# A hybrid of state-space scan, attention and mixture of experts: an attention order table, small transfers for the diagonals, a last product by chunk, and list products behind their codes

## The chip, the cores and the metric

The kernel runs on one core of a Trainium2 chip, as one launch. The metric is the device time of that launch in microseconds (us); less is better. The core has five instruction streams that run side by side and wait for each other by semaphores: TensorE (PE in the profile, its weight loads PEld), VectorE (DVE), ScalarE (ACT), GpSimd (POOL) and SyncE (SP). Each takes its own instructions in the order in which they were emitted. Nearly all plain transfers are issued from SP's queue, a few from ACT's, and gathers and scatters from POOL's.

## The reference, cut to what matters

The input is four images of 32x32 positions with 256 channels, in float32; in the reference below the tokens of an image are its 1024 positions.

```python
# layer 0: norm, projection to 512 channels, 3x3 depthwise convolution, gelu, selective scan
x = layernorm(src) @ w_in + b_in
x = gelu(depthwise_conv3x3(x) + conv_b)
dt_raw, B, C = split(x @ w_x)                 # 16, 64 and 64 columns
dt = softplus(dt_raw @ w_dt + dt_bias)
for t in tokens:                              # h: 512 channels x 64 states
    h = exp(dt[t] * A) * h + (dt[t] * x[t]) * B[t]
    y[t] = sum over the 64 states of h * C[t]
x = src + layernorm(y + x * D_skip) @ w_out + b_out
# layer 1: attention without a softmax over tokens, then experts
q, k, v = split(layernorm(t) @ W_qkv + b_qkv)  # q, k centred, squared and normalised to q2, k2
t = t + (v + q2 @ (k2.T @ v) / sqrt(N)) @ W_out + b_out
p = softmax(layernorm(t) @ gate_w + gate_b); the best two of 16 experts per token
t = t + sum of the two: weight * (silu(z @ w1) * (z @ w2)) @ w3
```

## The kernel before, in words

**Scan.** Layer 0 is cut into eight units, each half an image (512 tokens), and each unit into 64 steps, one for each state `n`. A step has four slots, one for each chunk `m` of 128 channels. In a slot ACT makes the decay `da` (`decay`), PE turns `dt*x*B` into a PSUM bank (`turn`), DVE runs the recurrence over 512 tokens (`scan`, L954), and PE adds the products with `C` up in PSUM (`add_up`, L975), eleven slots later (`LAG`). The product with `C` is one POOL instruction for all four chunks of a step (L961). The rows of `C`, called `cb_n`, are fetched three steps ahead by SP into four buffers (`fetch`, L880). The values that the next half image starts from go out by SP in a small transfer `last<-h` (L966). The work for the next units (norm, projection, convolution, `dt`) is fed into the slots from lists of pieces with a planned slot, which `beside` makes and the big loop under `tc.manual_schedule()` hands out.

The factor `B` can be multiplied in by ACT (`scale`), by POOL (`scale_apart`), or, for the first 128 tokens of some steps, by PE with a diagonal matrix. For that there are two DRAM tensors `diag_b[0]` and `diag_b[1]`, each 64 x 128 x 128. They are filled with zeros once (`zero_diagonals`, L252, in slots 4 and 14 of the first unit), and for each later unit `put_bc` writes the 64 x 128 entries of the diagonals, of 4 bytes each (L505). `fetch_diagonal` loads single matrices of it from the second unit on.

**Attention.** Layer 1 starts when the last scan has left PSUM. The order of its steps is a table, `ORDER`, of names with a batch and an index, which is run from front to back once; since every engine takes its instructions in the order of emission, the table sets each engine's order. The names that matter here:

- `st` are the statistics of one group of 128 tokens (DVE), `sc` scales half a batch by them (ACT, after a reciprocal on DVE), `tx` transposes it (PE), `qk` makes q and k (PE, then DVE and ACT), `vo` the part with v, `kv`, `ko`, `nk`, `kw` the matrix k2.T v and its scaling, `ou` the product with q2 and the statistics behind it.
- `ei` normalises half a batch for the experts into the tile `xe` (one buffer) and stores it to the DRAM tensor `xd` from SP; `te` and `ga` give the gate logits; `tg` and the `rs` steps choose the experts of a batch and find each token's place, a few DVE instructions each time; the weights of a batch's tokens go to `xd` from SP in one of them.
- `wr` writes a batch's rows to the output from ACT's queue. `nw` loads the weights of two experts into the memory of the finished batches' tiles `tb0`, `tb1`, `tb2` (names `m`), six transfers of 512 KB from SP in the order tb0, tb0, tb2, tb1, tb1, tb2. `fw` loads those of the first expert. `so` finishes the lists of the first three batches and gathers the first three blocks of rows.

**Experts.** The tokens are handled in 73 blocks of 128 rows (`blocks_of`). A block takes two halves of the hidden layer, 16 small matmuls each, named `p`, and two results `pf` (`hidden`, `result`). Beside the first eight blocks the rest of the routing is fed in, four pieces after each half block: `more_places` counts the blocks that experts with many tokens need beyond the fixed ones, and `more_rows` finds their rows. For these, DVE and ACT make a 0/1 `code` for eight groups of tokens at a time, eight codes in all, and PE multiplies each with the table `qh` in eight small matmuls (L2130). `more_places` also transposes a column `ef` on PE (L2085) from which DVE makes the expert numbers `eid`.

Of the kernel before, what the change touches and what calls it, by code (L numbers as in the profile page):

```python
# [22 lines left out]
def over_middle(ap, n):  # L23

    return ap.unsqueeze(1).to_broadcast([ap.shape[0], n, ap.shape[1]])
# [8 lines left out]
def conv_ssm_attn_moe_kernel(ctx: ExitStack, tc: tile.TileContext, a: dict, out: bass.AP):  # L34
# [110 lines left out]
    with ExitStack() as l0:  # L145
# [105 lines left out]
        def zero_diagonals(k):  # L251
            nc.sync.dma_start(  # L252
                out=diag_b[k].rearrange("n a b -> a n b"), in_=over_middle(zero, NS)
            )
# [200 lines left out]
        def dt_bc(w, needs):  # L455
# [42 lines left out]
            def put_bc():  # L498
                t = pre.tile([P, BANK], F32, name="bct")
                (nc.scalar.copy if on_scalar("bc") else nc.vector.tensor_copy)(t, made["bg"])  # L500
                cd = dram0.tile([NS, BANK], F32, name="cd")
                nc.sync.dma_start(out=cd, in_=t[NS:, :])
                if w > 0:
                    with nc.allow_non_contiguous_dma(reason="diagonals"):
                        nc.sync.dma_start(  # L505
                            out=diag_b[w % 2].rearrange("n a b -> n (a b)")[:, :: P + 1],
                            in_=t[:NS, :P],
                        )
                made["cd", w] = cd

# [125 lines left out]
            return parts + [todo]  # L636

# [308 lines left out]
        def scan(s, m):  # L946
# [12 lines left out]
            if m == DK - 1:  # L959
# [35 lines left out]
        def beside(u):  # L995
# [27 lines left out]
            if u + 1 < n:  # L1023
                lists.append(list(zip(dt_bc(u + 1, ("st", u - 1) if u > 0 else None), dts)))
            else:
# [67 lines left out]
        with tc.manual_schedule():  # L1093
# [14 lines left out]
            for k in range(n_all + LAG):  # L1108
# [13 lines left out]
                if k in (4, 14):  # L1122
                    zero_diagonals(1 if k == 4 else 0)
# [676 lines left out]
    def put_rows_out(b):  # L1800
# [14 lines left out]
        ('st', 0, 0), ('st', 0, 6), ('lt', 0), ('lt', 1), ('st', 0, 5), ('st', 0, 2), ('lp', 0),  # L1815
        ('lt', 2), ('st', 0, 1), ('st', 0, 3), ('sc', 0, 0), ('st', 0, 4), ('st', 0, 7),
        ('st', 1, 0), ('st', 1, 1), ('lp', 1), ('st', 1, 4), ('lt', 3), ('lp', 2), ('tx', 0, 0),
        ('lp', 3), ('sc', 0, 1), ('qk', 0, 0), ('st', 1, 2), ('tx', 0, 1), ('st', 1, 3),
        ('sc', 1, 0), ('qk', 0, 2), ('st', 1, 5), ('qk', 0, 5), ('qk', 0, 1), ('qk', 0, 3),
        ('f4', 0, 5), ('f4', 0, 0), ('st', 1, 6), ('qk', 0, 4), ('st', 1, 7), ('vo', 0, 0),  # L1820
        ('f4', 0, 2), ('f4', 0, 4), ('vo', 0, 4), ('k2', 0, 0), ('qk', 0, 6), ('tx', 1, 0),
        ('sc', 1, 1), ('f4', 0, 1), ('qk', 0, 7), ('vo', 0, 1), ('f4', 0, 7), ('tq', 0, 0),
        ('f4', 0, 3), ('st', 2, 0), ('f4', 0, 6), ('k2', 0, 1), ('st', 2, 5), ('qk', 1, 0),
        ('st', 2, 1), ('st', 2, 7), ('qk', 1, 1), ('tq', 0, 1), ('qk', 1, 2), ('f4', 1, 2),
        ('vo', 0, 2), ('st', 2, 2), ('ll',), ('tx', 1, 1), ('f4', 1, 0), ('kv', 0, 0),
        ('vo', 0, 7), ('st', 2, 6), ('qk', 1, 3), ('qk', 1, 4), ('vo', 0, 5), ('st', 2, 3),
        ('nq', 0), ('st', 2, 4), ('qk', 1, 5), ('kv', 0, 1), ('ls',), ('ko', 0), ('nk', 0),
        ('k2', 1, 0), ('kw', 0), ('co', 1), ('vo', 1, 1), ('sc', 2, 2), ('vo', 0, 6),
        ('ou', 0, 0), ('ou', 0, 1), ('vo', 0, 3), ('f4', 1, 1), ('ou', 0, 2), ('tx', 2, 0),
        ('qk', 1, 6), ('ou', 0, 3), ('f4', 1, 4), ('ou', 0, 6), ('vo', 1, 0), ('r3', 0),  # L1830
        ('ei', 0, 0), ('ou', 0, 4), ('f4', 1, 5), ('qk', 1, 7), ('st', 3, 0), ('f4', 1, 6),
        ('ou', 0, 7), ('k2', 1, 1), ('st', 3, 5), ('tq', 1, 0), ('ou', 0, 5), ('kv', 1, 0),
        ('f4', 1, 3), ('tq', 1, 1), ('wr', 0), ('f4', 1, 7), ('nq', 1), ('ei', 0, 1),
        ('qk', 2, 0), ('tx', 2, 1), ('vo', 1, 2), ('te', 0, 0), ('qk', 2, 1), ('st', 3, 1),
        ('te', 0, 1), ('st', 3, 2), ('f4', 2, 0), ('co', 0), ('st', 3, 6), ('ga', 0, 0),
        ('ga', 0, 1), ('st', 3, 4), ('vo', 1, 3), ('nk', 1), ('tg', 0), ('st', 3, 7), ('rs', 0),
        ('qk', 2, 2), ('kv', 1, 1), ('rs', 0), ('st', 3, 3), ('rs', 0), ('ko', 1), ('sc', 3, 2),
        ('rs', 0), ('vo', 1, 6), ('qk', 2, 3), ('f4', 2, 2), ('rs', 0), ('rs', 0), ('kw', 1),
        ('qk', 2, 4), ('f4', 2, 1), ('vo', 1, 4), ('rs', 0), ('ou', 1, 0), ('k2', 2, 0),
        ('rs', 0), ('f4', 2, 3), ('ou', 1, 2), ('qk', 2, 6), ('rs', 0), ('rs', 0), ('rs', 0),  # L1840
        ('ou', 1, 3), ('ou', 1, 4), ('vo', 2, 1), ('qk', 2, 5), ('ou', 1, 1), ('qk', 2, 7),
        ('vo', 1, 7), ('r3', 1), ('ei', 1, 0), ('k2', 2, 1), ('vo', 1, 5), ('f4', 2, 5),
        ('tx', 3, 0), ('rs', 0), ('ou', 1, 5), ('ou', 1, 7), ('rs', 0), ('vo', 2, 0), ('rs', 0),
        ('f4', 2, 4), ('vo', 2, 2), ('f4', 2, 7), ('rs', 0), ('te', 1, 0), ('kv', 2, 0),
        ('tq', 2, 0), ('rs', 0), ('ou', 1, 6), ('f4', 2, 6), ('qk', 3, 0), ('qk', 3, 1),
        ('tq', 2, 1), ('ei', 1, 1), ('vo', 2, 7), ('qk', 3, 2), ('ga', 1, 0), ('te', 1, 1),
        ('rs', 0), ('rs', 0), ('rs', 0), ('rs', 0), ('rs', 0), ('ga', 1, 1), ('tx', 3, 1),
        ('tg', 1), ('vo', 2, 4), ('rs', 1), ('rs', 1), ('rs', 0), ('rs', 1), ('wr', 1),
        ('kv', 2, 1), ('f4', 3, 0), ('rs', 1), ('ko', 2), ('nq', 2), ('nk', 2), ('rs', 1),
        ('qk', 3, 5), ('rs', 1), ('f4', 3, 1), ('rs', 1), ('kw', 2), ('qk', 3, 3), ('f4', 3, 3),  # L1850
        ('ou', 2, 0), ('vo', 2, 3), ('rs', 1), ('ou', 2, 4), ('qk', 3, 4), ('rs', 1),
        ('ou', 2, 1), ('k2', 3, 0), ('f4', 3, 4), ('ou', 2, 3), ('ou', 2, 2), ('rs', 1),
        ('r3', 2), ('qk', 3, 7), ('rs', 1), ('rs', 0), ('ei', 2, 0), ('vo', 2, 5), ('qk', 3, 6),
        ('rs', 1), ('ou', 2, 7), ('vo', 2, 6), ('ou', 2, 5), ('te', 2, 0), ('ou', 2, 6),
        ('f4', 3, 7), ('tq', 3, 0), ('ei', 2, 1), ('ga', 2, 0), ('rs', 1), ('vo', 3, 1),
        ('tq', 3, 1), ('f4', 3, 6), ('fw', 'w3'), ('rs', 1), ('vo', 3, 0), ('te', 2, 1),
        ('f4', 3, 2), ('k2', 3, 1), ('rs', 1), ('f4', 3, 5), ('rs', 1), ('rs', 1), ('vo', 3, 2),
        ('nq', 3), ('rs', 1), ('ga', 2, 1), ('kv', 3, 0), ('tg', 2), ('rs', 1), ('rs', 2),
        ('rs', 2), ('rs', 2), ('rs', 2), ('kv', 3, 1), ('nw',), ('ko', 3), ('wr', 2), ('rs', 2),
        ('rs', 2), ('rs', 2), ('rs', 2), ('nk', 3), ('fw', 'w2'), ('vo', 3, 4), ('rs', 2),  # L1860
# [203 lines left out]
    def more_places():  # L2064
# [37 lines left out]
        )  # L2102
        nc.vector.tensor_tensor(bh, bf, few, ALU.add)
        yield

    def more_rows(lo, hi):

        n = hi - lo
# [91 lines left out]
```

## Time and profile before

| | |
|---|---|
| median of 3 runs | 3352.31 us (3351.57 to 3356.69) |
| the profiled execution | 3350.39 us |
| its span, first to last instruction | 3348.6 us |
| PE, DVE, ACT, POOL busy | 3163.7, 2891.9, 2717.2, 2717.1 us |
| mean granted TensorE clock | 0.990 of full speed |

The busy times are unions over the span, and they are averages over stages with different limits. By the traces of the single instructions, the head of layer 0 lies at 0 to 128 us, the scan at 128 to 2682 us, attention at 2682 to 2910 us, and the experts from 2910 us to the end. In the profile's rows an engine is followed by the line of the kernel, the operation, the tile written and the tiles read, a count, the busy time and the idle time before it with the instruction or transfer that ended it. A granted clock of 1.00 is full speed.

### The profile page before, as it was taken

The numbers are of one execution on the slowest core, as the hardware profiler recorded it, in microseconds if no ns is written. First come the engines' busy times: TensorE is split into PE (matmuls) and PEld (weight loads), VectorE is DVE, ScalarE is ACT, GpSimd is POOL, SyncE is SP. The second block draws the span as 40 slices with busy tenths as digits, with TensorE's granted clock in tenths as the row PEclk, the third lists the DMA queues.
The fourth block names the chain that finished last, engine by engine and source line by source line (L and its number), as shares of the span: only waits on it lengthen the run. The fifth ranks groups of instructions, "written<-read, shape, count | busy, mean of one in ns | idle before, by whom it ended". The sixth has DMA issues, their size and how long they took to land. (4 is left out here: it accounts for less than half of the span.)

```text
span 3348.6 us, 62734 instructions
## 1 busy us (share of the span) xinstructions
PE 3163.7 (94%) x23407; PEld 2752.2 (82%) x23407; DVE 2891.9 (86%) x3435; ACT 2717.2 (81%) x4621; POOL 2717.1 (81%) x1215
## 2 busy tenths in 40 slices
PE   7899999999999999999999999989999999889998
PEld 4588888988899888888989888768778766689998
DVE  4699999999999999999999999999999978752222
ACT  1699999999999999999999999999999855422221
POOL 0388998999999989999999999999999943334443
PEclk9999999999999999999999999999999999899999
DMA  3542223224333232243333222422212121567785
GB/s 106 150 72 64 68 67 69 71 70 62 68 78 71 72 67 75 63 66 72 75 74 68 69 66 60 73 55 70 62 58 68 54 84 32 171 178 230 216 250 149
DMA packets 423835, 300.76 MB, mean 90 GB/s; under 512 B 225073, under 2 KB 329393, under 8 KB 423522
## 3 DMA queue, kind: packets, MB, share of 16 engines
q1 hardware_dynamic: 397202, 274.25, 31.8%
q0 software_dynamic: 14016, 18.05, 2.9%
q10 hardware_dynamic: 12304, 4.37, 0.5%
q8 instruction: 187, 3.06, 0.4%
q14 instruction: 126, 1.03, 0.1%
HBM read 262.34 MB, written 34.87 MB: 89 GB/s over the span
## 5 line engine op out<-in xcount | busy, mean ns | idle before, releaser
L961 POOL TENSOR_TENSOR h<-h,cb_n 128x2048 f32<-128x2048 f32 x512 | 2148.6, 4207 | 128.0 <-DVE h L954 79.7
L928 ACT ACTIVATE da<-dt,l_conv_a_log_sb 128x512 f32<-128x512 f32 x2048 | 1435.1, 712 | 21.1 <-DVE h L954 19.7
L908 ACT ACTIVATE bx<-dtxT,proj 128x512 f32<-128x512 f32 x1748 | 1243.4, 712 | 28.4 <-DVE dtxT L600 16.2
L975 PE MATMUL y<-ident,h 128*128 128x128 f32 x8192 | 1236.5, 274 | 9.1 <-POOL h L961 6.3
L954 DVE TENSOR_TENSOR_SCAN h<-da,last,ps 128x512 f32<-128x512 f32 x1024 | 1218.0, 1258 | 8.2 <-PE ps L940 2.8
L954 DVE TENSOR_TENSOR_SCAN h<-da,ps 128x512 f32<-128x512 f32 x1024 | 1169.4, 1200 | 30.3 <-ACT da L928 13.1
L940 PE MATMUL ps<-ident,bx 128*128 128x128 f32 x6992 | 1119.0, 276 | 39.9 <-DVE h L954 28.3
L975 PEld LDWEIGHTS y<-ident,h 128*128 128x128 f32 x8192 | 979.1, 141 | 99.9 <-issue 20.3
L940 PEld LDWEIGHTS ps<-ident,bx 128*128 128x128 f32 x6992 | 820.3, 142 | 99.3 <-DVE h L954 79.2
L1965 DVE TENSOR_TENSOR hT<-s,p 128x256 f32<-128x256 f32 x146 | 61.3, 420 | 282.3 <-ACT s L1964 282.3
L1983 POOL DMA_INDIRECT out_dram<-yb,src x73 | 116.0, 1589 | 211.1 <-DVE yb L1980 85.1
L940 PE MATMUL ps<-ident,bxp 128*128 128x128 f32 x800 | 236.7, 296 | 50.2 <-DVE h L954 37.3
L1964 ACT ACTIVATE s<-p 128x256 f32<-128x256 f32 x146 | 55.9, 383 | 267.0 <-PE p L1958 264.3
L413 PE MATMUL bg<-pad,dgc 128*128 128x256 f32 x864 | 258.2, 380 | 0.6 <-DMA dgc<-diags 0.6
L940 PEld LDWEIGHTS ps<-ident,bxp 128*128 128x128 f32 x800 | 112.0, 140 | 132.4 <-DVE h L954 78.9
L935 PE MATMUL ps<-dgb,dtxT 128*128 128x128 f32 x800 | 171.3, 296 | 21.6 <-DMA dgb<-diag_b 10.7
L919 POOL TENSOR_SCALAR bxp<-dtxT,proj 128x512 f32<-128x512 f32 x200 | 141.4, 707 | 58.8 <-DVE dtxT L600 58.8
L1958 PE MATMUL p<-xT,w 128*128 128x128 f32 x1408 | 173.4, 277 | 2.2 <-ACT xT L1938 2.2
L1958 PEld LDWEIGHTS p<-xT,w 128*128 128x128 f32 x1408 | 169.1, 193 | 5.2 <-ACT xT L1938 3.0
L935 PEld LDWEIGHTS ps<-dgb,dtxT 128*128 128x128 f32 x800 | 120.8, 191 | 48.9 <-DVE h L954 34.8
L413 PEld LDWEIGHTS bg<-pad,dgc 128*128 128x128 f32 x864 | 130.5, 191 | 0.8 <-DMA dgc<-diags 0.8
L1958 PE MATMUL p<-xT,m 128*128 128x128 f32 x928 | 115.3, 278 | 0.0
(342 smaller groups left out, 2671.9 us busy)
## 6 DMA issues: line engine op xcount, KB each, us to landing
cb_n<-cd SPq DMA_DIRECT2D x512, 256.0 KB, 3.3
m<-in_L_ffn_w_dram SPq DMA_DIRECT2D x87, 512.0 KB, 5.5
w<-in_L_ffn_w_dram SPq DMA_DIRECT2D x60, 512.0 KB, 7.3
dgc<-diags SPq DMA_DIRECT2D x84, 192.0 KB, 3.2
diag_b<-zero SPq DMA_DIRECT2D x2, 4096.0 KB, 16.6
dgb<-diag_b SPq DMA_DIRECT2D x100, 64.0 KB, 3.1
last<-h SPq DMA_DIRECT2D x256, 2.0 KB, 3.0
xd<-xe SPq DMA_DIRECT2D x8, 512.0 KB, 3.6
```

What stands on the lines that cost most here:

```text
L413: nc.tensor.matmul(made["bg"].rearrange("p (h w) -> p h w", w=WW)[:, blk(c, deep), :], made["dgc", m * 3 + i][:, j, :], pads[m][:, at : at ...
L908: nc.scalar.activation(t, made["dtxT", u][:, j, :], AF.Copy, scale=made["proj", u][:, j, R + n : R + n + 1])
L919: nc.gpsimd.tensor_scalar(t, made["dtxT", u][:, 0, :], made["proj", u][:, 0, R + n : R + n + 1], 1.0, ALU.mult, ALU.mult,)
L928: nc.scalar.activation(t, made["dt", u][:, m, :], AF.Exp, scale=A[:, m, n : n + 1])
L935: nc.tensor.matmul(t[:, blk(j, P)], made["dtxT", steps[s][0]][:, j, blk(m, P)], made["dgb", s], start=True, stop=True,)
L940: nc.tensor.transpose(t[:, blk(j, P)], made["bx", s, j][:, blk(m, P)], ident)
L954: nc.vector.tensor_tensor_scan(h[:, m, 1:], made.pop(("da", s, m)), made.pop(("dbx", s, m)), 0.0 if seg == 0 else last[b][:, n, m : m + 1] ...
L961: nc.gpsimd.tensor_tensor(h[:, :, :BANK], h[:, :, 1:], over_middle(made["c", s], DK), ALU.mult)
L975: nc.tensor.matmul(made["y", u][j][:, blk(m, P)], made["h", s][:, m, blk(j, P)], ident, is_transpose=True, start=n == 0 and m == 0, stop=n ...
L1958: nc.tensor.matmul(p12[:, j, s, :], w_of(w, key)[:, ck, blk(h + j, P)], on_b["xT", key][:, ck, :], start=(ck == 0), stop=(ck == CK - 1),)
L1965: nc.vector.tensor_tensor(on_b["hT", key][:, h : h + 2, :], s, p12[:, :, 1, :], ALU.mult)
L1983: s = nc.gpsimd.indirect_dma_start(of[:, :], bass.IndirectOffsetOnAxis(src[:, c : c + 1], 0), yb, None, bounds_check=NB * L - 1, oob_is_er ...
```

## The change

1. The zeros of the two diagonal tensors are written in sixteen transfers of eight matrices (512 KB) instead of two of 64 (4 MB), one in each of the first sixteen steps, those of `diag_b[1]` first.
2. The entries of a unit's diagonals are written in eight transfers of 8 x 128 elements instead of one of 64 x 128. They are pieces of their own, spread over the 40 slots from the planned start of `dt1`.
3. In the very last step of the scan, the product with `C` is made chunk by chunk, chunks 0 and 2 on POOL and 1 and 3 on DVE.
4. `ORDER` holds the same 332 entries in another order.
5. In `more_places` the transpose of `ef` and the making of `eid` come three pieces later, and in `more_rows` the matmuls of a code follow three codes behind it (`LATE`), with five buffers for the codes instead of two.

```diff
-        def zero_diagonals(k):
+        part_of = NS // 8
+
+        def zero_part(i):
+            k, n = 1 - i // 8, (i % 8) * part_of
             nc.sync.dma_start(
-                out=diag_b[k].rearrange("n a b -> a n b"), in_=over_middle(zero, NS)
+                out=diag_b[k][n : n + part_of].rearrange("n a b -> a n b"),
+                in_=over_middle(zero, part_of),
             )
...
-                if w > 0:
-                    with nc.allow_non_contiguous_dma(reason="diagonals"):
-                        nc.sync.dma_start(
-                            out=diag_b[w % 2].rearrange("n a b -> n (a b)")[:, :: P + 1],
-                            in_=t[:NS, :P],
-                        )
+                made["bct", w] = t
                 made["cd", w] = cd
+                done.add(("bct", w))
...
+        def entries(w):
+            def part(i):
+                with nc.allow_non_contiguous_dma(reason="diagonals"):
+                    nc.sync.dma_start(
+                        out=diag_b[w % 2].rearrange("n a b -> n (a b)")[
+                            blk(i, part_of), :: P + 1
+                        ],
+                        in_=made["bct", w][blk(i, part_of), :P],
+                    )
+            return [piece(4, "SP", 0, lambda i=i: part(i), need=("bct", w)) for i in range(8)]
...
-            if m == DK - 1:
+            if s + 1 == len(steps):
+                (nc.vector if m % 2 else nc.gpsimd).tensor_tensor(
+                    h[:, m, :BANK], h[:, m, 1:], made["c", s], ALU.mult
+                )
+            elif m == DK - 1:
...
+                lists.append([(entries(u + 1), (at["dt1"][0], at["dt1"][0] + 40))])
...
-                if k in (4, 14):
-                    zero_diagonals(1 if k == 4 else 0)
+                if k % DK == 2 and k // DK < 16:
+                    zero_part(k // DK)
...
     ORDER = (
-        ('st', 0, 0), ('st', 0, 6), ('lt', 0), ('lt', 1), ('st', 0, 5), ('st', 0, 2), ('lp', 0),
-        ('lt', 2), ('st', 0, 1), ('st', 0, 3), ('sc', 0, 0), ('st', 0, 4), ('st', 0, 7),
+        ('st', 0, 0), ('lt', 0), ('st', 0, 6), ('st', 0, 1), ('st', 0, 5), ('lt', 1),
+        ('st', 0, 2), ('st', 0, 3), ('lp', 0), ('st', 1, 0), ('lt', 2), ('sc', 0, 0), ('lp', 1),
...
-        ('nq', 3), ('rs', 1), ('ga', 2, 1), ('kv', 3, 0), ('tg', 2), ('rs', 1), ('rs', 2),
-        ('rs', 2), ('rs', 2), ('rs', 2), ('kv', 3, 1), ('nw',), ('ko', 3), ('wr', 2), ('rs', 2),
+        ('k2', 3, 0), ('nw',), ('rs', 1), ('vo', 2, 3), ('ou', 2, 3), ('qk', 3, 7), ('ou', 2, 2),
...
+        ('rs', 2), ('rs', 2), ('wr', 2), ('kv', 3, 1), ('ko', 3), ('rs', 1), ('rs', 2),
...
     )
...
         nc.vector.tensor_reduce(ef, done, AX.X, ALU.add)
-        pe = one()
-        nc.tensor.transpose(pe[:1, :P], ef, ident)
-        nc.vector.tensor_scalar(eid, pe[:1, :NMORE], float(NE - 1), None, ALU.min)
         yield
...
+            if k == 3:
+                pe = one()
+                nc.tensor.transpose(pe[:1, :P], ef, ident)
+                nc.vector.tensor_scalar(
+                    eid, pe[:1, :NMORE], float(NE - 1), None, ALU.min
+                )
             yield
...
+    LATE = 3
+
     def more_rows(lo, hi):
...
+        behind = []
+        def add_rows(k, c, code):
+            for j in range(GC):
+                nc.tensor.matmul(...)
...
                 yield
-                for j in range(GC):
-                    nc.tensor.matmul(...)
+                behind.append((k, c, code))
+                if len(behind) > LATE:
+                    add_rows(*behind.pop(0))
+        yield
+        for one_code in behind:
+            add_rows(*one_code)
```

## The prediction

> **What bounds the kernel now.** I read the page, then the engines' busy times by stage, then the waits and the time lines at the places that the edits touch.
>
> ```profile
> core 0: us, PE busy (x) PEld busy (x) DVE busy (x) ACT busy (x) POOL busy (x), PEclk, DMA share, GB/s
> 128.00:2682.00 2554.00, 2429.97 (x19000) 2157.93 (x19000) 2506.79 (x2299) 2475.31 (x3990) 2430.23 (x885) 1.00 0.30 70
> 2682.00:2910.00 228.00, 207.88 (x924) 144.01 (x923) 179.60 (x490) 117.87 (x358) 86.92 (x91) 0.97 0.26 82
> 2910.00:2980.00 70.00, 60.71 (x461) 54.91 (x462) 39.15 (x140) 19.41 (x43) 23.43 (x27) 0.92 0.66 186
> 2980.00:3338.00 358.00, 356.84 (x2710) 339.67 (x2708) 100.88 (x325) 73.22 (x193) 165.90 (x189) 1.00 0.75 218
> ```
>
> Each stage has its own limit. In the scan four engines are over 95% busy and DVE, at 98%, leads. Attention is PE's, at 91% with DVE behind. The first 70 us of the experts leave PE idle for 9.3 us at a clock of 0.92; after that PE has no room. So an edit pays where it closes a gap of the scan's DVE and ACT, of the join between scan and attention, or of PE at 2910 to 2980 us.
>
> **1. Zeros and entries.** SP's time line in the first steps of the scan:
>
> ```profile
> 133.78 0.62 SPq L252 DMA_DIRECT2D diag_b<-zero  x1
> 137.32 10.27 SPq L880 DMA_DIRECT2D cb_n<-cd  x1
> ...
> 151.56 0.57 SPq L252 DMA_DIRECT2D diag_b<-zero  x1
> 152.22 14.38 SPq L966 DMA_DIRECT2D last<-h  x1
> ```
>
> An issue on SP takes 0.3 to 0.7 us; behind each 4 MB of zeros the next ones take 10.27 and 14.38 us. SP stands still until the transfer has drained (16.6 us to landing), and `cb_n` and the image rows `xt` come late. ACT and DVE pay:
>
> ```profile
> ACT xn L327 <- DMA xt<-in_x_dram: 5.0, 1, 5.0
> ...
> 152.81 3.44 DVE L954 TENSOR_TENSOR_SCAN h<-da,ps 128x512 f32<-128x512 f32 x3 [2.02 <-PE ps L940]
> ...
> 169.18 4.55 DVE L954 TENSOR_TENSOR_SCAN h<-da,ps 128x512 f32<-128x512 f32 x4 [5.19 <-ACT da L928]
> ```
>
> With smaller gaps of 1.11, 0.52 and 0.50 us between these and up to 175 us, DVE loses 9.34 us here. ACT loses 5.02 + 0.77 = 5.8 us; between 230 and 260 us it waits for DVE for another 3.1 us, and from 300 to 450 us ACT never stops (149.9 of 150 us busy). So the gain is 5.8 us if ACT alone sets the pace later, and at most 5.8 + 3.1 = 8.9 us if DVE's lead closes ACT's later waits too. Now a part is an eighth of 16.6 us, 2.1 us of transfer in a step of about 4.7 us, beside one `cb_n` (3.3 us to landing). `xt` is then issued behind the third scan, at about 142.6 us, and with its own 4.8 us and one part ahead of it lands by 149.5 us; ACT asks for it at 150.6 us. No wait is left, and I take 8.0 us gained (5.5 to 9.3; nothing if small parts fill the queue as well).
>
> The entries: one transfer takes 13.3 us, and SP stands still 5.9 to 8.6 us behind the three that I looked at (194, 535, 826 us). But DVE has no gap over 0.4 us within 20 us of any of the seven. `cb_n` is fetched three steps (some 15 us) ahead, which hides it. Seven issues of 0.6 us become 56, each passing ahead of some `cb_n` or `last` on SP's queue: 30 us more on a queue that waits most of its time, an eighth of 13.3 us, 1.7 us, of transfer each. Without that cover each piece would delay a fetch by under 2 us. I take 0 (0.3 gained to 1 lost). The first diagonal is needed from the next unit on, over 100 slots later.
>
> **2. The last product.**
>
> ```profile
> 2669.84 5.95 DVE L954 TENSOR_TENSOR_SCAN h<-da,last,ps 128x512 f32<-128x512 f32 x5
> 2671.24 4.18 POOL L961 TENSOR_TENSOR h<-h,cb_n 128x2048 f32<-128x2048 f32 x1 [0.50 <-DVE h L954]
> 2672.83 4.61 PE L975 MATMUL y<-ident,h 128*128 128x128 f32 x40
> 2675.93 4.16 POOL L961 TENSOR_TENSOR h<-h,cb_n 128x2048 f32<-128x2048 f32 x1 [0.51 <-POOL h L961]
> 2680.14 1.97 PE L975 MATMUL y<-ident,h 128*128 128x128 f32 x16 [2.71 <-POOL h L961]
> 2682.32 0.31 POOL L1240 MEMSET none_t<- 128x258 f32 x1 [2.23 <-PE y L975]
> ```
>
> The last scan ends at 2675.79 us; product and sum follow one after the other to 2682.11, and `none_t`, which SP's loads of attention's input stand behind, starts only then. So all of attention moves with the sum. A chunk on POOL costs a quarter of 4.18, 1.05 us, or 1.3 us by the nearest 128x512 product (`two<-k`, L1377); I take 1.2. On DVE the nearest is `qk<-pqk,brow`, 0.69 us. If DVE's two products cost only that, scans end at 2676.5 and its last product at 2677.2; POOL's two end at 2677.8; PE, busy to 2677.44, adds four chunks by 2679.4: 2.7 us gained.
>
> A row speaks against this. At 2871.91 us a DVE product of two SBUF tiles took 1.42 us while POOL worked; the same size took 0.41 us after it:
>
> ```profile
> 2871.91 2.61 POOL L1383 TENSOR_TENSOR two<-two,k 128x512 f32<-128x512 f32 x2
> 2871.91 1.42 DVE L1529 TENSOR_TENSOR pr<-pr,m 128x128 f32<-128x128 f32 x1
> ...
> 2874.26 0.41 DVE L1534 TENSOR_TENSOR pr<-pr,m 128x128 f32<-128x128 f32 x1
> ```
>
> The Trainium skill, SBUF — State Buffer, "Who interferes with whom", has the rule: a DVE instruction with two SBUF inputs contends with a GpSimd instruction that reads SBUF, and the loser waits out the whole instruction. A scan takes one input from PSUM and is free of it; the new products (`h` and `cb_n`) are not. Chunk 1 is ready on DVE at 2673.4, but POOL's product of the step before holds on to 2675.42: 2.0 us in which scans 2 and 3 stand behind it. Then either DVE goes first and PE ends at 2679.7 (2.4 gained), or POOL's chunk does and it ends at about 2680.9 (1.2 gained). Without the rule 2.7, with it 1.2 to 2.4; I take 2.0.
>
> **3. The order table.** The work is the same; only what waits for what can change. By mean durations of its rows (`qk` 1.8 us on PE and 0.6 on DVE, `kv` 3.6 on PE for a half, `ou` 0.9 and 1.0, and so on) attention holds about 203 us of PE and 165 us of DVE. PE leads up to `kv` of batch 3, DVE behind it (no DVE gap over 0.4 us from 2843.7 to 2883 us), so the bound is PE's work up to a step plus DVE's from it on: 212.5 us at worst before (at `tg` 2) and 213.0 after (at `kv` 3 0). Two places can be read off. The table now has `st` 1 0 ahead of `sc` 0 0 on DVE: it needs `tb1`, whose landing the trace doesn't give, but its neighbours landed at 2689.26 and 2696.55, half way 2692.9. In the old frame `sc`'s reciprocal moves from 2692.41 to about 2693.5, and PE, which waits for it (2.18 us <- ACT xh), starts 1.1 us later. Near the end `kw` 3 has 0.9 us less DVE work ahead and `ei` 3 0 0.7 us more. Sum 0.5 + 1.1 - 0.9 + 0.7, about 1 us lost. The waits that I can't trace by hand (PE idles some 19 us in this stage) may close or open: 8 us either way.
>
> `nw` moves 50 places forward on SP. Its third load needs `tb2`, free when `wr` 2 has landed (2877.81 before). SP will now stand there for some 40 us, and behind it stand the weights of batch 1, `fw` w3 and both `xe` stores of batch 2. Nobody computes on these at once: the next to want the `xe` buffer is `ei` 3 0, on ACT at 2897.07, 19 us after that landing. Behind it go four loads and one, each some 1.45 us apart in landing (2883.21, 2884.57, 2886.02), then the stores: about 12 us. 7 us to spare; cost 0. `fw` w2 now goes right behind w1 (landed 2904.78) and lands about 1.5 us later, ahead of its use at 2909.88.
>
> **4. List products and `eid`.** PE's waits from 2940 to 2975 us, and its time line:
>
> ```profile
> PE one L2130 <- ACT code L2125: 4.9, 7, 1.7
> PE one L2085 <- DVE ef L2083: 1.9, 1, 1.9
> ...
> 2958.88 3.66 PE L1958 MATMUL p<-xT,m 128*128 128x128 f32 x16
> ```
>
> The first two are 6.8 us that PE stands. The last shows more: 16 matmuls `p` take 1.95 us elsewhere and 3.66 here, and the `pf` behind the last code's matmuls are slow again (four take 2.06, elsewhere 1.03). The clock halves for 3.4 us, twice, after gaps of no more than 1.67 us: 1.7 us lost, and by the `pf`, `px` and `p` at 2966 to 2969 us 1.7 again. The Trainium skill, TensorE: Matmul & The Clock Gate, "Why this matters for your kernels", puts the limit at gaps over about 3 us. By that rule nothing but the 6.8 us could be won; the trace shows short gaps in a row doing it, and it decides: 10.2 us could be won.
>
> Not all is. In the new order PE has one code's matmuls, 16 `p`, four codes' matmuls, `pf`, `px`, 16 `p`, `pf`, three codes'. DVE makes the first five codes without a break up to 2959.3 us and had 1.1 us of idle time before that, so they are done at 2958.2 at the earliest and PE is past them at 2958.6. What follows waits for nothing: 0.9 + 0.2 + 1.8 + 0.9 + 0.6 = 4.4 us, to 2963. Before, the same work ended at 2971.39. That is 8.4 us; I take 8.0, and 5.0 if the clock still halves. `eid` is read by SP for blocks over ten further on, and the five buffers hold all codes in flight.
>
> **Sum.** -8.0 + 0 - 2.0 + 1.0 - 8.0 = -17.0 us, against the profiled execution's 3350.4 us: 3333.4. The median of the runs is 1.9 us higher, so 3335.3, given as 3335.
>
> **The rivals.**
> - *The order costs* (15%): with 8 us more of PE waits in attention than summed, 3343 us. For it: `st` 1 0. Against: the two bounds differ by 0.5 us.
> - *The order gains* (17%): the tail's PE waits (3.88 us at `pc`, 3.34 at the gate) close; 8 us less, 3327 us.
> - *The parts don't do what they say* (8%): small zeros fill SP's queue as the big ones did, so part 1 gives nothing; 3343 us. Against: the stop came 3.5 us and 0.7 us behind 8192 small runs; a part has 1024.
> - *Slower* (5%): SP stands behind `nw`, and the `xe` stores come too late for `ei` 3 0. If its five loads went one after the other, each with the 7.3 us of the slowest median load, and not 1.45 us apart, the stores would be 29 us later, 22 more than there are to spare, and the time 3335 + 22 = 3357 us. It decides when the stores are 24 us later than I count, which passes 3352 us.
>
> **How the numbers follow.** The forecast has 55%, with 3329 to 3341 us from the bounds of parts 1, 2 and 4. Over all cases 8 in 10 lie in 3325 to 3345. A difference under 0.2%, 6.7 us, can't be told from none. The forecast and the gaining order are faster; the costing order and a failed part 1 (3343, 9 us below) are so in three of four cases: 0.88 faster, 0.07 the same, 0.05 slower.
>
> **What would show it.** Right: no SP issue over 3 us at 133 to 170 us and no DVE gap over 1 us there; from POOL's product of the last step but one (2671.24) to the end of the sum about 8.9 us, 10.9 before; the row `one<-code` loses most of its 4.9 us and `p` stays at 1.95 us for 16. Wrong: ACT still waits for `xt`; attention, from the first `tb` landing to the first `p`, over 225 us (222 before); ACT `xe` waiting for a store; `p` still at half clock.

## The result, and the profile after

| | before | changed |
|---|---|---|
| median of the runs | 3353.05 us (3351.57 to 3356.69, 5 runs) | 3336.55 us (3334.17 to 3339.68, 5 runs) |
| ratio, with its 95% interval | | 0.9949 [0.9935, 0.9964] |
| the profiled execution | 3350.39 us | 3336.55 us |
| its span | 3348.6 us | 3334.8 us |

The changed kernel is 16.5 us faster by the medians, where 17 were forecast. Stage by stage, from the two traces (each boundary is the start of the instruction named):

| stage | before | changed | difference | forecast |
|---|---|---|---|---|
| head, up to the first scan | 128.48 | 129.06 | +0.6 | 0 |
| first scan to POOL's product of the last step but one | 2542.76 | 2533.09 | -9.7 | -8.0 |
| from there to the end of the sum | 10.87 | 8.53 | -2.3 | -2.0 |
| end of the sum to the first statistics of attention | 5.79 | 5.59 | -0.2 | 0 |
| first statistics to the first `p` of the experts | 222.0 | 228.5 | +6.5 | +1.0 |
| first `p` to the end of the span | 438.7 | 430.0 | -8.7 | -8.0 |
| sum | 3348.6 | 3334.8 | -13.8 | -17.0 |

So each stage came out near its forecast but one: attention, where the order table acts, was badly mis-sized. By the profiled executions it adds up to -13.8 us; the profiled run of before lay 2.7 us under its median of five.

The busy times by stage of the changed kernel, to be held against those of before:

```profile
core 0: us, PE busy (x) PEld busy (x) DVE busy (x) ACT busy (x) POOL busy (x), PEclk, DMA share, GB/s
129.00:2671.00 2542.00, 2426.56 (x19000) 2156.78 (x19000) 2512.51 (x2301) 2474.29 (x3991) 2429.98 (x887) 1.00 0.28 70
2671.00:2905.00 234.00, 210.43 (x923) 144.77 (x924) 177.05 (x490) 118.01 (x358) 88.00 (x91) 0.96 0.25 80
2905.00:2975.00 70.00, 65.52 (x531) 59.87 (x532) 41.58 (x148) 20.92 (x47) 26.09 (x30) 0.97 0.78 225
```

In the scan DVE does its work (2512.5 us of it) in 2542 us instead of 2554. Attention is longer, with more PE time for the same matmuls. In the first 70 us of the experts PE idles 4.5 us instead of 9.3, at a clock of 0.97 instead of 0.92.

SP's time line in the first steps, where 10.27 and 14.38 us stood before:

```profile
137.90 0.32 SPq L893 DMA_DIRECT2D cb_n<-cd  x1
138.27 0.44 SPq L255 DMA_DIRECT2D diag_b<-zero  x1
138.75 0.60 SPq L983 DMA_DIRECT2D last<-h  x1
...
143.93 1.25 SPq L321 DMA_DIRECT2D xt<-in_x_dram  x1
...
152.89 1.89 SPq L983 DMA_DIRECT2D last<-h  x1
```

No issue up to 160 us takes over 1.89 us, `xt` goes out at 143.9 us, and DVE has no gap over 0.3 us from 129 to 250 us. The end of the scan, POOL's and DVE's time lines:

```profile
2662.15 4.18 POOL L978 TENSOR_TENSOR h<-h,cb_n 128x2048 f32<-128x2048 f32 x1 [0.50 <-POOL h L978]
2666.29 2.95 POOL L973 TENSOR_TENSOR h<-h,cb_n 128x512 f32<-128x512 f32 x2
2670.88 0.31 POOL L1258 MEMSET none_t<- 128x258 f32 x1 [1.64 <-PE y L992]
...
2664.40 2.48 DVE L973 TENSOR_TENSOR h<-h,cb_n 128x512 f32<-128x512 f32 x1
2666.80 2.44 DVE L967 TENSOR_TENSOR_SCAN h<-da,last,ps 128x512 f32<-128x512 f32 x2
2669.28 0.69 DVE L973 TENSOR_TENSOR h<-h,cb_n 128x512 f32<-128x512 f32 x1
```

DVE's first product takes 2.48 us and ends, at 2666.88 us, only after POOL's big product has (2662.15 + 4.18 = 2666.33); its second, the same instruction, takes 0.69. Behind attention, PE's waits from 2905 to 2980 us (row: waiting engine, tile and line, what it waited for, us in all, times, longest), and then one line of its time line:

```profile
PE one L2138 <- ACT code L2161: 1.8, 4, 1.0
PE one L2111 <- DVE ef L2101: 0.2, 1, 0.2
```

```profile
2948.88 2.05 PE L1976 MATMUL p<-xT,m 128*128 128x128 f32 x16
```

Of 4.9 + 1.9 us, 2.0 remain, and the 16 matmuls `p` at this place take 2.05 us instead of 3.66: the clock does not halve.

### The profile page after: what moved, and what is told of

Its sections match the earlier page's. It is cut to its first block, busy times and chain, and to the rows that moved or that the text cites. A ratio compares the mean times of both kernels' runs of the same rounds, so it can differ in the third digit from the quotient of the medians.

```text
span 3334.8 us, 62828 instructions
## 1 busy us (share of the span) xinstructions
PE 3158.7 (95%) x23407; PEld 2747.8 (82%) x23407; DVE 2895.5 (87%) x3437; ACT 2716.5 (81%) x4621; POOL 2718.2 (82%) x1216
## 4 chain that ended last, share of the span: by engine, by line
ACT 42%; PE 37%; DVE 11%; issue 4%; POOL 3%; DMA 2%; SPq 0%; DVEq 0%; POOLq 0%; ACTq 0%
ACT da L941 21%; ACT bx L921 18%; DVE h L967 7%; PE ps L953 7%; PE p L1976 7%; PE y L992 7%; PE pf L1991 3%; PE bg L417 3%; POOL h L978 2%; PE ps L417 2%; PE pqk L1354 1%; PE ps L948 1%; PE ps L364 1%; DMA dgb<-diag_b 1%; PE bg L470 0%
```

## The experiments

They were made in four groups, each on one chip with the kernel before beside it. The median of the kernel before was 3353.04 us in the first group, and 3364.12, 3364.89 and 3365.18 us in the other three; why it is 11 to 12 us slower there is taken up under part 1. So each time is held against the kernels of its own group, or the traces are compared.

### Part 1: zeros and entries

**The zeros alone** (first group, on the kernel before):

```diff
-                out=diag_b[k].rearrange("n a b -> a n b"), in_=over_middle(zero, NS)
+                out=diag_b[k][n : n + part_of].rearrange("n a b -> a n b"),
+                in_=over_middle(zero, part_of),
...
-                if k in (4, 14):
-                    zero_diagonals(1 if k == 4 else 0)
+                if k % DK == 2 and k // DK < 16:
+                    zero_part(k // DK)
```

> The kernel before with the zeros of the diagonals in sixteen small transfers, nothing else. Theory (SP's standstill behind the two 4 MB transfers cost DVE 9.3 us, and all of it is won since ACT catches up): the product of the last step but one ends 9.5 us earlier, near 2661.7 in the trace, and the time is 9 to 9.7 us under before, 3343 us. Rival (ACT sets the pace later, so only its own 5.8 us are won, and the remaining 3 to 4 us of the 9.7 seen are the small entries' doing): 3347 us.

Measured: 3346.29 us median (3341.39 to 3359.38, 19 runs), ratio 0.9977 [0.9971, 0.9984]: 7.7 us by the ratio (6.8 by the medians), with 5.4 to 9.7 in the interval. Neither theory is right as it stands. In its trace the scan is 8.7 us ahead of before's by POOL's ninth product and 9.5 by the fifteenth: ACT did not hold it to 5.8. But at 204 us it falls back by 2.6 us, and the changed kernel does not. SP's time line and DVE's next scans of this kernel, and then SP's in before:

```profile
188.84 0.60 SPq L509 DMA_DIRECT2D diag_b<-bct  x1
189.49 8.59 SPq L255 DMA_DIRECT2D diag_b<-zero  x1
198.18 1.68 SPq L970 DMA_DIRECT2D last<-h  x1
...
204.19 2.33 DVE L958 TENSOR_TENSOR_SCAN h<-da,ps 128x512 f32<-128x512 f32 x2 [2.55 <-DMA last<-h]
```

```profile
193.71 0.60 SPq L505 DMA_DIRECT2D diag_b<-bct  x1
194.41 8.57 SPq L966 DMA_DIRECT2D last<-h  x1
```

SP stands 8.59 us behind the one transfer of entries. `last<-h` reads the step's tile `h`, of which there are four in a ring (`RING = 4`), so the scan four steps on must wait until it has landed. By the landings in the traces, `last<-h` landed 13.2 us after the entries were issued in before (206.93 us), and DVE was ready for that scan 13.4 us after them: 0.2 us to spare. Here it landed 15.2 us after them (204.07), with a part of the zeros issued in between, and DVE was ready after 12.8. So 2.0 of the 2.55 us fit the part in between, and 0.6 the shorter steps. At the three later transfers of this kind, with no zeros in between, DVE is still 7 to 8 us ahead and waits 0, 0 and 0.41 us, and in before 0, 0 and 0.28. That DVE is ahead is thus not what makes it wait; a run with the zeros out of the way of that one `last<-h` was not made.

The profiled execution was also the slowest of the 19 (3359.38 us), and by the last products its scan is just 0.3 us ahead of before's; what took the gain is told at the end.

**Zeros and entries together** (second group, on the kernel before): besides the edit above

```diff
-                if w > 0:
-                    with nc.allow_non_contiguous_dma(reason="diagonals"):
-                        nc.sync.dma_start(
...
+                made["bct", w] = t
...
+                lists.append([(entries(u + 1), (at["dt1"][0], at["dt1"][0] + 40))])
```

> The kernel before with the zeros and the diagonals' entries in small transfers (part 1 whole), nothing else. With the zeros alone the scan was 9.5 us ahead by the fifteenth product and lost 2.6 us again at 204 us, where DVE waited for last<-h, queued on SP behind the entries' single transfer. Theory (once DVE is early, the single entry transfer comes on the path, so the small entries are worth 2.6 us and not 0): no DVE gap at 204 us, 9.5 us kept, 3343.5 us, some 2.7 under the zeros alone. Rival (the wait at 204 us was chance): 3346 us, like the zeros alone.

Measured: 3344.33 us against 3364.12, ratio 0.9945 [0.9932, 0.9958], 19.8 us. There is no DVE gap at 204 us, and the 9.5 us are kept. So the single transfer was needed for that wait, as the theory says, though not because DVE is early. (The edit also spreads the entries over later slots, from 203 us on instead of 189; small and later were not tried apart.) But 19.8 is twice what the theory allowed: on this chip the kernel before loses more than zeros can explain.

**The entries alone** (third group). The first kernel is the changed one with the old order table, run as the measure; the second puts the one transfer of entries back into it.

> The changed kernel with the order table of before once more, as the measure for the next run on the same chip. Theory (the table's cost of 6 us holds anywhere): attention near 222 us and 3329 to 3331 us.

> The changed kernel with the order table of before and the entries of a unit's diagonals in one transfer again, as before. Theory (behind each of the seven transfers SP stands 8 to 10 us, last<-h goes out late, and DVE's scan waits for it, since DVE now runs ahead): DVE gaps before h<-da with releaser last<-h near 200, 835, 1475 and 2115 us, 2.5 us in all where the standstill is 8.5 us long and 10 us where it is 10 long, so 3 to 10 us slower than the same kernel with small entries: 3333 to 3340 us. Rival (the entries are hidden, as summed beforehand): no such gaps, 3330 us.

Measured: 3333.14 us with small entries, 3348.62 with one transfer (0.9903 [0.9889, 0.9918] and 0.9952 [0.9939, 0.9965] of before): the small entries are worth 15.5 us here. DVE's waits in the scan, first with one transfer, then with eight:

```profile
DVE h L973 <- DMA last<-h: 11.4, 4, 4.7
DVE h L973 <- ACT da L947: 9.7, 18, 1.9
DVE h L973 <- PE ps L959: 8.8, 40, 0.5
DVE dt L558 <- PE bg L547: 3.8, 2, 2.7
```

```profile
DVE h L967 <- PE ps L953: 9.2, 43, 0.3
DVE h L967 <- ACT da L941: 7.6, 17, 1.9
DVE h L967 <- ACT bx L921: 2.1, 8, 0.6
```

One of the places, in SP's and DVE's time lines of the kernel with one transfer:

```profile
2098.93 0.61 SPq L509 DMA_DIRECT2D diag_b<-bct  x1
2099.63 10.09 SPq L989 DMA_DIRECT2D last<-h  x1
...
2115.89 4.55 DVE L973 TENSOR_TENSOR_SCAN h<-da,ps 128x512 f32<-128x512 f32 x4 [4.71 <-DMA last<-h]
```

SP stands 10.1 us here; in the profiled execution of before it stood 8.3 to 9.2 us behind the same four transfers, and `last<-h` then cost DVE 0.5 us in the whole scan. The landing has three steps of scans, some 14 us, to be in time: with before's standstill it was, by 0.2 and 0.6 us at 194 and 825 us, or just was not (0.3 us late at 2101 us); with 10 us it is not. The waits stand at 202 (with a part of the zeros in between again), 1476 and 2116 us, with 1.5 us of ACT's at 836: always in the first half of an image, where `last` is written at all. The measure, 3 to 10 us, was too small, since `dt` behind the last of these waits for PE another 3.8 us. An early DVE is not needed for it: in the second group a kernel that differs from before in the last product alone (below), with the large zeros and a scan that is not ahead, waits 2.1, 1.4, 3.0 and 3.8 us for `last<-h` at 209, 842, 1484 and 2123 us, behind standstills of 10.0 to 10.5 us. That is also why before is 11 us slower in these groups, while the changed kernel with the old table is only 3.2 us slower than in the first. (For the fourth group it is an inference: no kernel with the single transfers was profiled there.)

**The zeros from ACT's queue** (second group):

```diff
-            nc.sync.dma_start(
+            nc.scalar.dma_start(
                 out=diag_b[k].rearrange("n a b -> a n b"), in_=over_middle(zero, NS)
```

> The kernel before with its two 4 MB transfers of zeros issued from ACT's queue instead of SP's; their size is unchanged. Theory (what hurts is that SP's queue stands still behind 8192 runs of 512 bytes, not that the DMA engines are busy): no SP issue over 3 us at 133 to 170 us, DVE's gaps of 9.3 us at 150 to 175 us go, the eighth product of the scan comes 8.7 us earlier as in the changed kernel, and 6 to 9 us are won, 3344 to 3347 us. Rival A (the transfers themselves keep the 16 DMA engines busy, so that cb_n and xt land late from whatever queue): the gaps stay, 3353 us. Rival B (ACT stands behind its own issue as SP did, 10 us each): slower than before, 3357 us or more.

Measured: 3362.17 us against 3364.12, ratio 0.9997 [0.9989, 1.0006]: nothing. The trace tells why. No SP issue up to 150 us takes over 1.34 us, with 4 MB of zeros under way, so rival A is out: what stands still is the queue that issued them, not the DMA engines. But ACT has both zeros in its own stream, and stands itself, as rival B said:

```profile
152.20 0.37 ACTq L252 DMA_DIRECT2D diag_b<-zero  x1
152.62 0.72 ACT L908 ACTIVATE bx<-dtxT,proj 128x512 f32<-128x512 f32 x1 [6.83 <-DMA diag_b<-zero]
```

The second transfer holds ACT for 6.83 us until the first has drained, and DVE, short of `da`, waits 4.80 us. By the ninth product 2.3 us are won instead of 8.7, and 2.0 of them go again at 206 us.

### Part 2: the last product

**By chunk, alone on the kernel before** (second group):

```diff
-            if m == DK - 1:
+            if s + 1 == len(steps):
+                (nc.vector if m % 2 else nc.gpsimd).tensor_tensor(
+                    h[:, m, :BANK], h[:, m, 1:], made["c", s], ALU.mult
+                )
+            elif m == DK - 1:
```

> The kernel before with the last product of the scan by chunk, two on POOL and two on DVE, nothing else. Theory: from POOL's product of the last step but one to the end of the sum 8.5 us instead of 10.9, DVE's first product near 2.5 us beside POOL's, the second 0.7, and 2.3 us won, 3350.7 us; too little to be told from no change by the times, so the trace's 8.5 us decide. Rival (part of the 2.3 us seen in the changed kernel came from POOL being earlier for another reason): 9.5 us or more.

Measured: 8.52 us, DVE's products 2.48 and 0.69 us, as the theory says (3364.06 us against 3364.12, 0.9996 [0.9987, 1.0005], not to be told apart by time). All eight kernels with this split take 8.52 to 8.54. The kernels with one product take 10.87 in before, but 12.15 to 12.33 in the four others: there the 16 matmuls that wait 2.7 us for the product run slower afterwards (3.25 to 3.44 us, 1.97 in before). So the split is worth 2.3 to 3.8 us.

**All four chunks on POOL**, on the changed kernel (second group): `nc.gpsimd.tensor_tensor(` for every `m`.

> The changed kernel with all four products of the last step's chunks on POOL, none on DVE. Theory (DVE's first product waits for POOL's product in progress, so DVE's share buys little): the scans follow each other without DVE's 2.5 us, each product on POOL takes 1.1 to 1.3 us, and from POOL's product of the last step but one to the end of the sum it takes 8.5 to 9.6 us; the time 3336.5 to 3337.5 us. Rival (the split is worth what two DVE products of 0.7 us beside two POOL products of 1.2 would give): 10.4 us or more and 3338.5 us.

Measured: 9.43 us; POOL's time line:

```profile
2667.31 4.58 POOL L973 TENSOR_TENSOR h<-h,cb_n 128x512 f32<-128x512 f32 x4
```

DVE's share buys 0.9 us, not the 1.9 of the rival; the time is 3337.04 us (0.9926 [0.9913, 0.9938] of its before). Of the 2.3 us of part 2, the chunks alone bring 1.4.

### Part 3: the order table

**The old table in the changed kernel** (first group; again in the third, above):

> The changed kernel with the order table of before; nothing else differs. Theory (the new table costs what the two traces show): attention, from the first tb statistics to the first p, comes back from 228.5 to about 222 us, and the time is 6.5 us under the changed kernel's 3336.5, near 3330 us. Rival A (the table costs 1 us, as summed beforehand, and the other 5.5 us come from the earlier start of attention itself, with a clock and loads that stand otherwise): attention stays near 227.5 us, the time near 3335.5. Rival B (what attention lost, the first PE gap of the experts gave back): 3336.5, no change.

Measured: 3329.98 us (3328.83 to 3336.34), ratio 0.9937 [0.9924, 0.995]; attention takes 222.3 us. The theory holds: the table costs 6.6 us by the medians (4 us by the two ratios to before, whose intervals overlap, so the traces must bear it out). In the third group the same comparison, against the kernel with `nw` back below, gives 3337.21 - 3333.14 = 4.1 us. Over all traces, attention takes 222.0 to 225.8 us with the old table (nine kernels, mean 224.1) and 228.3 to 229.9 with the new one, or the new one with one entry moved (four, mean 229.1): 5.0 us, with no overlap. This kernel is the fastest of all that ran, and faster than both given ones.

PE's time line at the start of attention, the changed kernel and then this one:

```profile
2683.08 2.79 PE L1298 MATMUL ps_t<-ident,xh 128*128 128x128 f32 x8 [3.50 <-ACT xh L1336]
2685.66 3.62 PE L1319 MATMUL po_l<-l_conv_w_out_sb,yT 128*128 128x256 f32 x8
2689.07 2.44 PE L1354 MATMUL pqk<-wqk,xhT 128*128 128x512 f32 x4
```

```profile
2679.91 2.32 PE L1298 MATMUL ps_t<-ident,xh 128*128 128x128 f32 x8 [1.84 <-ACT xh L1336]
2682.07 1.89 PE L1319 MATMUL po_l<-l_conv_w_out_sb,yT 128*128 128x256 f32 x8
2683.80 1.88 PE L1354 MATMUL pqk<-wqk,xhT 128*128 128x512 f32 x4
```

In the changed kernel DVE waits for `tb1` before `st` 1 0, ahead of the reciprocal that `sc` needs:

```profile
2681.78 0.43 DVE L1281 BATCH_NORM_STATS2 ln_st<-tb 128x6 f32<-128x256 f32 x1 [1.45 <-DMA tb<-td]
...
2682.34 0.14 DVE L1288 RECIPROCAL ln_rs<-ln_rs 128x4 f32<-128x4 f32 x1
```

PE starts 6.8 us after the first statistics instead of 5.2, and after its longer gap eight `po_l` take 3.62 us instead of 1.89. By the first `qk` on DVE 4.2 us are lost (15.3 us after the first statistics, 11.0 here). It looks like the whole answer.

**Only that entry moved** (first group):

```diff
-        ('st', 0, 2), ('st', 0, 3), ('lp', 0), ('st', 1, 0), ('lt', 2), ('sc', 0, 0), ('lp', 1),
+        ('st', 0, 2), ('st', 0, 3), ('lp', 0), ('lt', 2), ('sc', 0, 0), ('st', 1, 0), ('lp', 1),
```

> The changed kernel with one entry of the table moved: st 1 0 stands behind sc 0 0 instead of two entries ahead of it. Theory (the wait of st 1 0 for tb1 holds up sc's reciprocal, PE starts 1.3 us late and then works at half clock): the first DVE qk comes about 11 us after the first tb statistics, not 15.3, and 3 to 4 us are won, 3332.5 to 3333.5 us. Rival A (the half clock comes from something else at that place, only the wait of 1.4 us goes): 3335 us. Rival B (attention's end is set by the second half of the table, so a faster start is taken up by later waits): 3336.5 us, first p still 228 us after the first statistics.

Measured: 3335.83 us, ratio 0.9956 [0.9942, 0.997]. The first `qk` comes after 12.6 us instead of 15.3. That is inside the 11.0 to 13.5 us of the nine kernels with the old table, so the start is mended; but attention still takes 228.3 us. Rival B holds: the start's loss is not attention's. PE's time line at that place, where a wait of 2.12 us is enough to slow the matmuls behind it (2.75 us for the eight `po_l`, 1.89 above):

```profile
2681.49 2.78 PE L1298 MATMUL ps_t<-ident,xh 128*128 128x128 f32 x8 [2.12 <-ACT xh L1336]
2684.06 2.75 PE L1319 MATMUL po_l<-l_conv_w_out_sb,yT 128*128 128x256 f32 x8
```

The loss shows as idle time of DVE. Up to the first `kvw` of batch 3, DVE stands idle for 35.5 to 37.9 us in all nine kernels with the old table, and 41.3 to 43.2 in the four with the new one. Nothing is given back behind it: from there to the first `p` it takes 26.1 to 28.6 us with the old table and 29.4 to 29.6 with the new one.

**A second entry moved as well** (fourth group). The largest new DVE gap stood behind the gate's matmuls, PE's and DVE's time lines of the kernel just told:

```profile
2758.72 4.67 PE L1528 MATMUL pgT<-xeT,l_ffn_gate_w_sb 128*16 128x512 f32 x8
2763.32 1.09 PE L1298 MATMUL ps_t<-ident,xh 128*128 128x128 f32 x8
...
2764.01 1.29 DVE L1299 COPY xhT<-ps_t 128x512 f32<-128x512 f32 x2 [4.07 <-PE ps_t L1298]
```

So `tx` 2 1 went ahead of them:

```diff
-        ('ei', 0, 1), ('qk', 2, 0), ('st', 3, 3), ('te', 0, 0), ('qk', 2, 1), ('st', 3, 4),
+        ('ei', 0, 1), ('qk', 2, 0), ('tx', 2, 1), ('st', 3, 3), ('te', 0, 0), ('qk', 2, 1), ('st', 3, 4),
...
-        ('ga', 0, 1), ('tx', 2, 1), ('tg', 0), ('rs', 0), ('rs', 0), ('st', 3, 6), ('co', 0),
+        ('ga', 0, 1), ('tg', 0), ('rs', 0), ('rs', 0), ('st', 3, 6), ('co', 0),
```

> The kernel with st 1 0 behind sc 0 0 and, besides, tx 2 1 directly behind qk 2 0 instead of behind the gate steps te and ga of batch 0; the rest of the new order table stays. Theory (the new table lets DVE stand 5 to 6 us longer before kv of batch 3, of it some 4 us where PE makes 4.7 us of gate matmuls ahead of tx 2 1): the wait of xhT for ps_t, 4.07 us, goes, DVE stands 37 to 38 us instead of 41.3 up to the first kvw of batch 3, attention takes 225 to 226 us instead of 228.3, and the time is 333x: 2.5 to 3 us less, near 3333. Rival (as with st 1 0, later waits take the gain up): DVE's idle time stays at 41 us, attention at 228 us, 3336 us.

Measured: 3336.53 us (0.992 [0.9906, 0.9933] of its before), attention 231.6 us, DVE idle for 45.3 us up to that `kvw`. A miss: the wait moved to the next two readers of PE's work.

```profile
2759.53 0.69 DVE L1359 TENSOR_TENSOR qk<-pqk,brow 128x512 f32<-128x512 f32 x1 [3.51 <-PE pqk L1354]
...
2766.73 0.29 DVE L1542 TENSOR_TENSOR pr<-pg,l_ffn_gate_b_row 128x128 f32<-128x128 f32 x1 [3.84 <-PE pg L1537]
```

No single entry carries the cost; which stretch of the table does stays open.

**`nw` put back** behind `kv` 3 1 (third group):

> The changed kernel, new order table, with the one entry nw back behind kv 3 1. Theory (SP's stand behind nw is covered, and what the new table costs sits on DVE's and PE's order): attention stays at 228 us, no ACT wait for a store, 3336.5 us. Rival (the early nw costs, by the late xe stores or by its transfers beside attention's): attention 3 us shorter or more, 3333 us or less.

Measured: 3337.21 us (0.9916 [0.9903, 0.9929] of its before), attention 229.9 us, no ACT wait for a store. Attention is no shorter for it, so the early `nw` is not what the table costs. (By time this can't be told: the changed kernel did not run in this group.)

### Part 4: the lists

On the kernel before (first group), the diff's last part alone: `eid` three pieces later, `LATE = 3` and five buffers.

> The kernel before with the list products three codes behind and eid later, nothing else. Theory (6.8 us of PE's waits and about 1.7 us of half clock go): from the first p to the end of the span 430 us, not 438.7, and the time 8.5 us under before, 3344 us. Rival A (the clock halves again, since after the other waits the gaps in a row remain): 5 us under before, 3347.5. Rival B (part of the 8.7 us seen in the changed kernel came from attention's new end, which hands over with more lists ready): under 5 us won, 3348 us or more.

Measured: 3343.8 us, ratio 0.997 [0.9959, 0.9982]. From the first `p` to the end of the span it takes 430.4 us; before 438.7, and the changed kernel 430.0. Both rivals, at 5 us or less, lie outside the interval of the times (6.0 to 13.7 us gained) and outside the trace's 8.3.

## Why the prediction was right, and where it was wrong

The total, 3335 us, lies 1.6 us under the measured 3336.55. So close a hit is partly luck: the profiled executions, which the terms were summed for, differ by 13.8 us and not by 17.0, and one of the signs named for being wrong, attention over 225 us, came true (228.5). The steps behind it:

- **Zeros, -8.0: right in mechanism, a little small.** SP's standstill caused the gaps, and small parts end it. 9.5 us came, all of DVE's gaps (9.34 us by the forecast's own sum) and above the 8.9 that was set as the most from ACT's waits. The term that failed is that bound: ACT's stretch without a stop, at 300 to 450 us, was no limit, as the gain was there by 212 us and still there at the end.
- **Entries, 0: the step that failed without showing.** The cover named was `cb_n`, three steps ahead. The transfer in danger was `last<-h`, which stood directly behind the entries in two of the lines that were read, and whose reader is the ring of four `h`. "DVE has no gap over 0.4 us within 20 us of any of the seven" held (but for 0.50 us at 174 us, 19.5 us ahead of the first), yet with as little as 0.2 us to spare, and that depends on the standstill and on what else is issued in between. With the small zeros and one transfer of entries, the wait was 2.6 us where a part of the zeros came in between and SP stood 8.6 us, and the small entries were worth 15.5 us where it stood 10. "Without that cover each piece would delay a fetch by under 2 us" priced the new version, not the old one.
- **The last product, -2.0: right.** The rule of the Trainium skill, "SBUF — State Buffer", "Who interferes with whom", decided the number: 2.48 us beside POOL against 0.69 alone. Without it 2.7 us were forecast, with it 1.2 to 2.4; 2.34 came, and the 8.5 us in every kernel with the split.
- **The order, +1.0: the mis-sized step, +4 to +6.6.** `st` 1 0 was read rightly (1.1 us forecast, 1.45 of wait and 1.5 of PE's start measured), but it was not what cost: mended, it gave attention nothing. The bound from busy times (212.5 against 213.0 us) treated PE as packed up to the crossing and then DVE; it could not see that DVE stands 5 to 6 us longer before the crossing. PE is busy for longer too, but little: 206.1 to 207.1 us with the new table, 202.9 to 206.5 with the old one for the same matmuls; the start shown above has 1.7 us of it. The reference of 222.0 us was also the lowest of nine. Which stretch of the table makes DVE stand stays open.
- **`nw`, 0: right**, by the kernel with `nw` back and by the trace: the `xe` stores went out at 2876 and 2879 us, and ACT did not wait.
- **The lists, -8.0: right**, 8.3 to 8.7, for the reasons given. The clock question was decided as the trace of before had it: with the waits in a row gone, `p` is at full clock again. The waits fell from 6.8 to 2.0 us, which is 4.8; the matmuls that had been slow (`p`, `pf`, `px`, `p`) took 5.5 us instead of 8.7, which is 3.2 more. The Trainium skill, "TensorE: Matmul & The Clock Gate", "Why this matters for your kernels", with its limit of gaps over about 3 us, would have allowed the waits alone; 8.3 speaks against it for gaps in a row. For single gaps the runs put the limit lower as well: at the start of attention 3.50 us did halve the clock, but 2.12 us slowed the matmuls too, and of the five gaps of 2.70 us before the sum of an undivided last product four did.

The rival "the order costs" describes what the order did, at 4 to 6.6 us instead of 9; the total stayed near the forecast because part 1, product and lists together gave 2.8 us more than taken, and because the profiled run of before lay 2.7 us under its median.

## What to carry to other kernels

A transfer of 8192 small runs stopped the queue that issued it, so ask of each such one what stands directly behind it, and how long that may be late; the answer changes when another edit puts one more transfer in between, and it differed from chip to chip here, with 0.2 us of slack on one and a standstill 1.5 us longer on the others. That a wait doesn't show in a trace means that it is covered there, not that it is free. For an order table, a bound by busy times is too weak: mending its most visible wait gave nothing, and mending the next made another.

## What was not expected of the hardware

- The queue stops behind small runs whatever they carry: 4 MB in 8192 runs of 512 bytes held the next issue 10.27 and 14.38 us, 32 KB in 8192 elements of 4 bytes held it 5.8 to 9.2 us, and 7.3 to 10.8 us on another chip. The same zeros from ACT's queue left SP free and held ACT 6.83 us.
- A DVE instruction of two elements a partition can wait for several POOL instructions in a row. The scan has three of the kind, which scale column means of attention's weights (`w_mean` twice, `b_mean`). In the trace of before, POOL's and then DVE's time lines:

```profile
2214.58 8.31 POOL L961 TENSOR_TENSOR h<-h,cb_n 128x2048 f32<-128x2048 f32 x2
2222.85 1.27 POOL L584 TENSOR_TENSOR e<-e,s 128x512 f32<-128x512 f32 x1
2224.07 4.16 POOL L961 TENSOR_TENSOR h<-h,cb_n 128x2048 f32<-128x2048 f32 x1
2228.18 1.27 POOL L586 TENSOR_TENSOR e<-e,dtxT 128x512 f32<-128x512 f32 x1
...
2220.18 9.30 DVE L762 TENSOR_SCALAR w_mean<-w_mean 128x2 f32<-128x2 f32 x1
2229.39 5.72 DVE L954 TENSOR_TENSOR_SCAN h<-da,ps 128x512 f32<-128x512 f32 x5
```

It ends at 2229.48 us, when POOL's unbroken run of instructions ends (2229.45), and three POOL instructions that were started after it are done before it. The same instruction takes 9.3 to 9.4 us in thirteen of the fourteen traces; in that of the changed kernel it takes 7.4, and the first `w_mean` another 5.7, where elsewhere that takes 0.3 to 0.4. So DVE, which leads in the scan, stands some 9 us here in every kernel, before and changed. None of the edits touched it, the forecast did not see it, and what it would bring to be rid of it was not tried. In the trace of the zeros alone `b_mean` was caught as well:

```profile
2248.72 8.02 DVE L766 TENSOR_SCALAR b_mean<-b_mean 128x2 f32<-128x2 f32 x1
```

It takes 0.2 to 0.9 us in the thirteen other traces. Here the scan, 8.3 us ahead of before's until then, fell back by 8.4 us: that is the gain of the zeros in that execution. All sixteen that took over 5 us end within 0.03 us of the end of POOL's run. The Trainium skill, "SBUF — State Buffer", "Who interferes with whom", names `tensor_scalar` among the operations that can take the ports shared with GpSimd, and lets the loser wait for one whole instruction; here it waited for up to five. DVE's first product of part 2, with two SBUF inputs, got in between two of them: it ended 0.6 us after POOL's big product, and POOL's next chunk took 1.72 us where the one behind it took 1.09. Why the one gets in and the other does not, the runs don't show.
